# A four-stage block on one core: gates, scaling and table switches reordered in six places

## The chip, the cores and the metric

The kernel runs on one core of a Trainium2 chip. The metric is the device time in microseconds of one execution; smaller is better. Times given are medians of several runs. One further execution was recorded by the hardware profiler, and all durations of single instructions come from it.

## The reference, cut to what matters

The input x has 4 rows of 512 tokens with 512 channels in fp32. A side input f of the same shape drives four gates. The reference is two layers of two steps each:

```python
x = x + mamba2(gate(x, f, f, w0, u0, cond))        # L0: attn
x = x + experts(gate(x, f, f, w1, u1, cond))       # L0: 8 experts, top 2, with gate
x = x + attention(gate(x, f, f, w2, u2, cond))     # L1: 16 heads in 4 groups, causal
x = x + ffn(gate(x, f, f, w3, u3, cond))           # L1: silu(g) * u, 1408 wide

def gate(r, k, v, w, u, time_emb):                 # k = v = f
    decay = exp(-exp(w)) * (0.5 + 0.5 * tf)        # one number per row and channel
    ek = exp(min(k, 30)); ekv = ek * v
    # scans over the tokens, forwards and backwards, of ekv and of ek
    num = nf + nb - ekv + exp(min(u + k, 30)) * v
    den = df + db - ek + exp(min(u + k, 30))
    return sigmoid(r) * num / max(den, 1e-8) * (0.8 + 0.2 * tf)

# mamba2: z, xBC, dt = h @ in_proj; xBC = silu(conv4(xBC)); y by chunks with
# cumulative sums of dA = softplus(dt) * A; then
y = y * silu(z)
y = y * rsqrt(mean(y * y) + eps) * norm_w
return y @ out_proj.T
```

Everything of a gate except sigmoid(r) depends on f alone, so a gate's quotient can be made long before x is there.

## The kernel before, in words

Channels or tokens lie on the 128 partitions; every product is an fp32 matmul of 128 by 128 with up to 512 columns. The program is written as one stream, and a scheduler orders each engine's instructions from it. `after(engine, ...)` pins what is inside it behind the last instruction issued so far on those engines. The class `Tables` (`act`) does the same for ScalarE's function tables: `act.use(name)` issues a table load behind everything recorded under the old table, and each call `act(...)` is pinned behind the load. A raw `nc.scalar.activation` is not pinned, and where it meets another table the compiler puts a load in front of it.

**Gates.** `gate_pair` makes the quotient of two chunks of 128 channels of one row as a generator: loads and Exp of k (`keys`), ek times k (`products`), a forward scan (L256) and a backward scan (L262) for the numerator and for the denominator, the bonus with exp(u + k) (L273 to L277), Ln and Exp for the reciprocal on ScalarE, three operations of 128x1024 on VectorE (L319, L323, L328), and for all but row 0 of the first gate a store of 512 KB to memory (L330, on SP's queue). A row of one gate is two pairs. `make_gates` interleaves consecutive pairs; `pump()` runs it up to its next mark, five marks to a pair, `nudge()` runs it one step. `gated` loads the stored quotient and multiplies it by tanh(x / 2) + 1; `have` first pumps until that gate is made. The list for the second layer is the four rows of gate 2, then the four of gate 3.

**Start.** Row 0's first gate is made from the beginning: its two pairs run six steps each, issued one pair after the other in the program and interleaved by the scheduler. The weights wxb, wzt and wot (2 MB, L926) are loaded; POOL makes the diagonal tiles `skip` (L921). Then each pair is finished, multiplied by the tanh (L1275), and its half of the products of the first eight chunks is issued (`conv_products`, L1007). Taps on ScalarE and VectorE (L1022) follow, `time_steps` (dt and dA, small operations on VectorE), and `sums`: three products of dA with triangles (ppr), Exp, a copy cs (L991), a transpose of cs on TensorE (pcs, L993), its copy csT (L995) and a store, from which the tiles lm are loaded again, spread over partitions.

**Rows.** For each row b and each tile t of 128 tokens: `start_tile`, `start_scores`, `decays`, `outputs`, `squares`, `norm`, and for the tile before (`old`) `turn`, `project`, `scale`, `add_x`. `turn` transposes y and multiplies by norm_w as it leaves PSUM: the first four of eight blocks by one VectorE operation (L1219), the others by four on ScalarE (L1227). `project` multiplies by wot (L1235). One table switch to Silu and one back is in each tile. `pump` makes the later gates of layer 0 in between, and `routing` steps through `choose_experts` (gate 1, logits) and `route` for the row before: ranks and slots by small VectorE operations and products such as ptok (L576), whose two inputs ov and os are built on VectorE. The tables that `route` needs (lane, res_id, place, v_lo, v_e) are made on POOL and VectorE near the beginning (L437 to L464).

**Experts.** Token rows are gathered by expert into blocks. `moe.round()` does one block: products pg, pn and po (L775, L786, L808) with weights loaded on SP's queue, 3 MB a block at most. From block 17 on, two slots of weights alternate. In `more`, each round is followed by one `pump()`, now for the second layer's gates, until block NBLK - 4. Then the results of row 0 are combined with x (L1454 to L1464).

**Attention.** Four groups of 4 heads; for each group, 4 rows; 64 heads in all. `begin` issues the products of the next head, `scores` the softmax of a head (mask L1585, maximum L1587, a nudge of the gates, Exp L1592 as raw activation, L1593, L1594), `context` and `dense` the rest. In group 0, at the second head of row b, the results of row b + 1 are combined and its gated input is made (`gated(2, b + 1)`). Then the FFN, by rows, with its Silu at L1700.

Of the kernel before, what the change touches and what calls it, by code (L numbers as in the profile page):

```python
# [80 lines left out]
def block_kernel(ctx: ExitStack, tc: tile.TileContext, a: dict, out: bass.AP):  # L81
# [354 lines left out]

    lane = count("lane", [[1, P]])  # L437

    res_id = [count(f"res{c}", [[TOPK * T, B], [P, NT]], 1, 1 + c * T) for c in range(2)]
    for r in res_id:  # L440
        for b in (0, B - 1):
            rb = r[:, b * NT : (b + 1) * NT]
            nc.vector.tensor_scalar(rb, rb, float(AT[b] - b * TOPK * T), None, ALU.add)

    places = tmp.tile([P, NBLK], I32, tag="th", name="places")
    for lo, hi in ((0, FIRST), (FIRST, NBLK - NEARLY)):
        half = (hi - lo + 1) // 2
        nc.gpsimd.iota(places[:, lo : lo + 2 * half], pattern=[[1, half], [half, 2]], base=lo,  # L450
                       channel_multiplier=0)
    place = rt.tile([P, NBLK - NEARLY], F32, name="place")
    nc.vector.tensor_copy(place, places[:, : NBLK - NEARLY])
    e_nq = count("e_nq", [[NQ, E]])
    v_id = count("v_id", [[1, 1]], 1)

    v_lo = rt.tile([P, 1], F32, name="v_lo")
    v_e = rt.tile([P, 1], F32, name="v_e")
    jk = rt.tile([P, E], F32, name="jk")
    nc.vector.tensor_tensor(jk, sel, e_nq, ALU.mult)  # L460
    nc.vector.tensor_reduce(v_e, jk, AX.X, ALU.add)
    nc.vector.tensor_tensor(v_lo, v_id, v_e, ALU.subtract)
    nc.vector.tensor_scalar(v_lo, v_lo, float(P), None, ALU.mult)
    nc.vector.tensor_scalar(v_e, v_e, 1.0 / NQ, 1.0 - E, ALU.mult, ALU.add)  # L464


# [39 lines left out]

    def route(lg, b, fine):
        n = NT * E
# [56 lines left out]
        yield  # L565
        pt = ps_tp("ptok")
        over = lambda v: v.unsqueeze(2).to_broadcast([P, NT, P])
        lanes = lane.unsqueeze(1).to_broadcast([P, NT, P])
        for c, (q, s_) in enumerate(vq):
            ov = tmp.tile([P, NT, P], F32, tag="th", name="ov")  # L570
            nc.vector.tensor_tensor(ov, lanes, over(q), ALU.is_equal)
            nc.vector.tensor_tensor(ov, ov, over(res_id[c][:, bt_]), ALU.mult)
            os_ = tmp.tile([P, NT, P], F32, tag="th", name="os")
            nc.vector.tensor_tensor(os_, lanes, over(s_), ALU.is_equal)
            for t in range(NT):
                nc.tensor.matmul(  # L576
                    pt[:, :P], lhsT=ov[:, t, :], rhs=os_[:, t, :],
                    start=(t == 0 and c == 0), stop=(t == NT - 1 and c == 1),
                )
# [15 lines left out]
    def choose_experts(b, xb, parts, pool, fine=False, **kw):  # L595

        lg = rt.tile([P, NT, E], F32, tag="lg", name="lg", bufs=2)
        nt = NT // parts
        for i in range(parts):
            h = gated(1, b, xb, pool, slice(i * nt * P, (i + 1) * nt * P), **kw)  # L600
            if fine:
                yield
            logits(h, b, lg, i * nt, nt)
            yield
        yield from route(lg, b, fine)

# [254 lines left out]
    with ExitStack() as ph:  # L861
# [23 lines left out]
        def lend_halves():  # L885
# [9 lines left out]
        lent = [  # L895
            {"f": lend("y", 3), "eu": lend("tmp", 2)},
            {
# [5 lines left out]
        pairs = [gate_pair(0, 0, c0, first, lent[c0 // 2]) for c0 in range(0, NC, 2)]  # L903
        for pair in pairs:
            for _ in range(6):
                for _ in step(pair):
                    pass
        x = {0: load_x(0)}
        turned, lend_turned = [], lend_halves()
        for cc in range(NC):  # L910
            turned.append(lend_turned())
            act(turned[cc], x[0][:, cc, :], AF.Tanh, scale=0.5)
        act.use(act.LOG_EXP)
        NX = DPROJ - DI
        wxb = wx.tile([P, NC, NX], F32, name="wxb")
# [8 lines left out]
        for k in range(NC):  # L924
            nc.sync.dma_start(out=wzt[:, k, :], in_=a["in_projT"][k * P : (k + 1) * P, :DI])
        nc.sync.dma_start(out=wot, in_=a["out_projT"].rearrange("(k p) m -> p k m", p=P))  # L926

        def time_steps(w):
# [44 lines left out]
        def sums(w):  # L973
# [14 lines left out]
            nc.vector.tensor_tensor(dte, dt, ex[:, 1], ALU.mult)  # L988

            cs = sm.tile([P, n], F32, tag="cs", name="cs", bufs=2)  # L990
            nc.vector.tensor_copy(cs, pp[:, :n])  # L991
            pcs = ps_tp("pcs")
            nc.tensor.transpose(pcs[:n, :P], cs, ident)  # L993
            csT = four[:n, 0:2, :].rearrange("p i t -> p (i t)")
            nc.vector.tensor_copy(csT, pcs[:n, :P])  # L995
            nc.sync.dma_start(out=cs_d[w.b], in_=csT)
# [213 lines left out]
        def turn(u):  # L1210

            u.yT = sm.tile([P, NDI, P], F32, tag="yT", name="yT")
            for hh in range(2):
                pyt = ps_tp("pyt")
                for j in range(4):
                    js = slice(j * P, (j + 1) * P)
                    nc.tensor.transpose(pyt[:, js], u.y[hh][:, js], ident)
                if hh == 0:
                    nc.vector.tensor_tensor(  # L1219
                        u.yT[:, :4, :],  # L1220
                        pyt.rearrange("p (j t) -> p j t", t=P),
                        col("norm_w", 0, 4).unsqueeze(2).to_broadcast([P, 4, P]),
                        ALU.mult,
                    )
                else:
                    for j in range(4):
                        nc.scalar.mul(  # L1227
                            u.yT[:, 4 + j, :], pyt[:, j * P : (j + 1) * P], col("norm_w", 4 + j)
                        )

# [63 lines left out]
        load_sums(w, 0, 1)  # L1294
        decays(u, 0)
        old = None
        routing = iter(())
        for b in range(B):
# [6 lines left out]
            for t in range(NT):  # L1305
# [86 lines left out]
                with after(*ENGINES):  # L1392
                    next(routing, None)
                    if b == B - 1 and t == 1:
                        next(routing)
# [75 lines left out]
    with tc.tile_pool(name="moe_w2", bufs=1, reuse_waits="tile") as wm:  # L1471
# [4 lines left out]
        def more(limit):  # L1476
            while moe.i < min(limit, moe.known):
                moe.round()
                if moe.i < NBLK - NT:
                    with after(nc.vector):  # L1480
                        pump()

# [28 lines left out]
    with att as ph:  # L1511
# [64 lines left out]
        def scores(u, i, qT):  # L1576

            prs = []
            for qi in range(NT):
# [11 lines left out]
                rsum = sm.tile([P, 1], F32, tag="rsum", name="rsum", bufs=4)  # L1591
                nc.scalar.activation(pr, psc[:, :n], AF.Exp, bias=nmax, accum_out=rsum)  # L1592
                nc.vector.reciprocal(rsum, rsum)  # L1593
# [50 lines left out]
        def begin(n):  # L1644
# [5 lines left out]
            return groups[g, b], queries(groups[g, b], i)  # L1650

        groups = {}
        ready, held = begin(0), None
        for n, (g, b, i) in enumerate(heads_):
            u, qT = ready
            if g == 0 and i == 1 and b + 1 < B:
                combine(b + 1)
                hs[b + 1] = gated(2, b + 1, x[b + 1], gp, tag="h", name=f"h2_{b + 1}")
            if n + 1 < len(heads_):
                ready = begin(n + 1)  # L1660
            prs = scores(u, i, qT)
            if held is not None:
# [7 lines left out]
        for _ in making:  # L1670
            pass


    with ExitStack() as ph:
# [9 lines left out]
        for b in range(B):  # L1684
            h = gated(3, b, x[b], gp, tag="h", name=f"h3_{b}")
            hd = []
            for i in range(NFF):
# [11 lines left out]
                hi = sm.tile([P, T], F32, tag="hd", name="hd", bufs=NFF + 2)  # L1699
                nc.scalar.activation(hi, pg, AF.Silu, scale=col("gate_s", i))  # L1700
                nc.vector.scalar_tensor_tensor(hi, pu, col("up_s", i), hi, ALU.mult, ALU.mult)  # L1701
# [85 lines left out]
```

## Time and profile before

| | |
|---|---|
| median of 3 runs | 2587.08 us (2586.99 to 2592.27) |
| profiled execution | 2591.44 us, span 2589.7 |
| mean granted TensorE clock | 0.978 |
| TensorE busy | 2446.0 us |
| VectorE, ScalarE, POOL busy | 1409.8, 1032.3, 250.4 us |
| table loads on ScalarE | 68 of 1.283 us |
| stores of gate quotients (L330) | 30 of 512 KB, five of them in 860 to 1180 us |

The stages lie one behind the other: start to about 100 us, rows to about 750, experts to about 1180, attention to about 2140, FFN to the end. In these rows, "busy" is the time in which an engine executes; a wait is an idle time of an engine just before an instruction, and "<-" names what released it. "PEclk" is the clock that TensorE was granted, in tenths. In the timeline, the first column is the start in us from the span's start, the second the duration, and a bracket at the end gives the idle time before.

### The profile page before, as it was taken

To read this page: it belongs to the slowest core of one execution; us is meant where nothing else is said; L and a number is where in the kernel's file an instruction comes from. 1 tells how busy PE (TensorE), PEld (TensorE's weight loads), DVE (VectorE), ACT (ScalarE), POOL (GpSimd) and SP (SyncE) were. 2 spreads that over 40 slices of the span, in tenths; PEclk is the share of its full clock that TensorE was granted. 3 is DMA by queue.
4 is the path that set the end of the run, shared out by engine and by line. 5 is a ranking of instruction groups with operands and counts; after the bars stand their busy time and mean duration, and the time that the engine had idled before them with its cause. 6 is when DMAs were issued, how large, how long until landed. Compare 5 with 4: busy or idle time off the path is not lost.

```text
span 2589.7 us, 24584 instructions
## 1 busy us (share of the span) xinstructions
PE 2446.0 (94%) x8204; PEld 1301.0 (50%) x8204; DVE 1409.8 (54%) x2786; ACT 1032.3 (40%) x2129; POOL 250.4 (10%) x301
## 2 busy tenths in 40 slices
PE   3889998999999999999989999999999999999999
PEld 1555555556544444445545555555555554444444
DVE  8789998997335555646686554556544441010010
ACT  4666756657222333325554444344443431000000
POOL 1031323313211111120000000000000000000000
PEclk9979998999899999999999999999999999999999
DMA  6222523324244697745231101110000012000000
GB/s 217 77 94 76 188 69 112 131 80 159 66 175 140 223 337 283 274 177 163 75 92 46 46 27 29 45 45 30 21 25 17 17 69 82 17 0 16 8 8 16
DMA packets 88510, 244.09 MB, mean 94 GB/s; under 512 B 9536, under 2 KB 19136, under 8 KB 79296
## 3 DMA queue, kind: packets, MB, share of 16 engines
q1 hardware_dynamic: 79200, 215.78, 24.3%
q0 software_dynamic: 6880, 22.55, 2.5%
q10 hardware_dynamic: 2304, 4.20, 0.4%
q8 instruction: 65, 1.06, 0.2%
q14 instruction: 61, 0.50, 0.1%
HBM read 284.82 MB, written 47.05 MB: 128 GB/s over the span
## 4 chain that ended last, share of the span: by engine, by line
PE 75%; DVE 16%; ACT 4%; DMA 3%; issue 1%; POOL 0%; SPq 0%; ACTq 0%; DVEq 0%
PE pd L1629 8%; PE pq L1565 7%; PE pfu L1696 6%; PE pfo L1706 6%; PE pfg L1691 6%; PE pctx L1614 5%; PE po L808 5%; PE pg L775 5%; PE pn L786 5%; PE psc L1582 3%; PE pc L1007 2%; PE po L1235 2%; PE pv L1551 2%; PE ptp L1605 2%; PE pz L1078 2%; PE pk L1543 2%
## 5 line engine op out<-in xcount | busy, mean ns | idle before, releaser
L1565 PE MATMUL pq<-h,wq 128*128 128x512 f32 x512 | 248.0, 600 | 10.9 <-ACT pr L1592 10.9
L1629 PE MATMUL pd<-cx,wd 128*128 128x512 f32 x512 | 222.9, 593 | 1.3 <-DVE xr L1637 1.3
L1007 PE MATMUL pc<-h,wxb 128*128 128x512 f32 x320 | 151.6, 629 | 46.1 <-DVE h L1275 39.0
L1700 ACT ACTIVATE hd<-pfg,cols 128x512 f32<-128x512 f32 x44 | 30.3, 688 | 380.8 <-PE pfg L1691 380.8
L1701 DVE SCALAR_TENSOR_TENSOR hd<-pfu,cols,hd 128x512 f32<-128x512 f32 x44 | 33.0, 751 | 269.1 <-PE pfu L1696 269.0
L1585 DVE TENSOR_TENSOR psc<-psc,mask 128x128 f32<-128x128 f32 x256 | 72.2, 288 | 192.9 <-PE psc L1582 192.9
L1592 ACT ACTIVATE pr<-psc,nmax 128x128 f32<-128x128 f32 (+3 forms) x256 | 135.5, 530 | 95.6 <-DVE nmax L1587 94.9
L1614 PE MATMUL pctx<-pT,v 128*128 128x512 f32 (+3 forms) x512 | 153.6, 443 | 8.5 <-ACT pT L1608 5.1
L1696 PE MATMUL pfu<-h,ffu 128*128 128x512 f32 x352 | 158.7, 592 | 0.8 <-DMA ffu<-in_upT 0.8
L1691 PE MATMUL pfg<-h,ffg 128*128 128x512 f32 x352 | 158.6, 592 | 0.0
L1582 PE MATMUL psc<-kT,qT 128*128 128x128 f32 (+3 forms) x512 | 153.1, 439 | 3.1 <-ACT qT L1573 1.6
L1629 PEld LDWEIGHTS pd<-cx,wd 128*128 128x128 f32 x512 | 95.9, 190 | 116.8 <-issue 110.0
L1706 PE MATMUL pfo<-hd,ffd 128*128 128x512 f32 x352 | 151.7, 592 | 0.0
L775 PE MATMUL pg<-w,hT 128*128 128x512 f32 x312 | 144.7, 606 | 4.3 <-DMA w<-in_w1x 4.3
L1614 PEld LDWEIGHTS pctx<-pT,v 128*128 128x128 f32 x512 | 93.4, 190 | 99.6 <-issue 35.9
L808 PE MATMUL po<-w,yT 128*128 128x512 f32 x312 | 142.3, 596 | 1.2 <-DMA w<-in_w2x 1.2
L786 PE MATMUL pn<-w,hT 128*128 128x512 f32 x312 | 140.7, 592 | 0.0
L1637 DVE TENSOR_TENSOR xr<-xr,pd 128x512 f32<-128x512 f32 x64 | 44.0, 687 | 169.3 <-PE pd L1629 169.3
L1587 DVE TENSOR_REDUCE nmax<-psc 128x1 f32<-128x128 f32 (+3 forms) x256 | 124.0, 486 | 2.6
L1007 PEld LDWEIGHTS pc<-h,wxb 128*128 128x128 f32 x320 | 62.6, 201 | 119.6 <-issue 73.8
L1565 PEld LDWEIGHTS pq<-h,wq 128*128 128x128 f32 x512 | 87.1, 192 | 69.4 <-issue 56.1
L1605 PEld LDWEIGHTS ptp<-ident,pr 128*128 128x128 f32 x640 | 77.8, 142 | 87.4 <-issue 38.4
(308 smaller groups left out, 4220.2 us busy)
## 6 DMA issues: line engine op xcount, KB each, us to landing
w<-in_w1x SPq DMA_DIRECT2D x80, 1024.0 KB
w<-in_w2x SPq DMA_DIRECT2D x40, 1024.0 KB
wb<-in_b1x SPq DMA_DIRECT2D x40, 512.0 KB
lm<-cs SPq DMA_DIRECT2D x32, 512.0 KB
kt<-in_fT SPq DMA_DIRECT2D x62, 256.0 KB
ek<-ek SPq DMA_DIRECT2D x62, 256.0 KB
ekv<-ekv SPq DMA_DIRECT2D x62, 256.0 KB
g<-num SPq DMA_DIRECT2D x30, 512.0 KB
```

The source lines that it names most:

```text
L775: nc.tensor.matmul(pg, lhsT=hT[:, k, :], rhs=self.w1[s][0][:, k, :], start=(k == 0), stop=(k == NC - 1))
L786: nc.tensor.matmul(pn, lhsT=hT[:, k, :], rhs=self.w1[s][1][:, k, :], start=(k == 0), stop=(k == NC - 1))
L808: nc.tensor.matmul(po, lhsT=yT[:, j, :], rhs=self.w2[s][:, j, :], start=(j == 0), stop=(j == NI - 1))
L1007: nc.tensor.matmul(pc, lhsT=wxb[:, k, m * P : (m + 1) * P], rhs=h[:, k, :], start=(k == 0), stop=(k == NC - 1),)
L1565: nc.tensor.matmul(pq, lhsT=u.wq[:, k, i * KVC : (i + 1) * KVC], rhs=u.h[:, k, :], start=(k == 0), stop=(k == NC - 1),)
L1582: nc.tensor.matmul(psc[:, :n], lhsT=qT[:, qi * P : n], rhs=u.kT[:, :n], start=True, stop=True)
L1592: nc.scalar.activation(pr, psc[:, :n], AF.Exp, bias=nmax, accum_out=rsum)
L1614: nc.tensor.matmul(pctx[:, kj * P :], lhsT=u.v[:, kj, :], rhs=pT[:, kj, kj * P :], start=(kj == 0), stop=(kj == NT - 1),)
L1629: nc.tensor.matmul(po, lhsT=u.wd[:, i, m * P : (m + 1) * P], rhs=u.ctxT[i], start=(i == 0), stop=(i == HPG - 1),)
L1691: nc.tensor.matmul(pg, lhsT=wg[:, k, cs], rhs=h[:, k, :], start=(k == 0), stop=(k == NC - 1))
L1696: nc.tensor.matmul(pu, lhsT=wu[:, k, cs], rhs=h[:, k, :], start=(k == 0), stop=(k == NC - 1))
L1706: nc.tensor.matmul(po, lhsT=wdn[:, i, m * P : (m + 1) * P], rhs=hd[i], start=(i == 0), stop=(i == NFF - 1),)
```

## The change

It has seven parts.

1. The tables of the routing are made behind the first tile's first `decays` on VectorE instead of near the beginning.
2. Row 0's first pair of the first gate is finished, on VectorE's order, before the second pair's six steps are issued. Its ekv tiles are lent from another pool.
3. wot is multiplied by norm_w once, by eight POOL operations of 128x512. `turn` then only copies, one ScalarE operation of 128x512 for each half.
4. In `sums`, the transposed cumulative sums come from a fourth product with dA in place of a transpose of cs.
5. In `route`, for the rows that are routed in fine steps, ov and os of the first half are made in a tile of another pool, and a step ends there; the PSUM tile of ptok is taken behind it. The last row's loop therefore takes an additional routing step at two tiles instead of one.
6. In the experts' stage, `pump` is called with one and two by turns.
7. In the attention, Exp goes through `act` under the table that also holds Ln; the table is loaded at its start. `gated(2, b + 1)` moves from the second head to the third, behind `begin`, between two table switches. The FFN's Silu goes through `act`, its table asked for at the end of the attention.

```diff
@@ route
-        pt = ps_tp("ptok")
+        pt = None
         for c, (q, s_) in enumerate(vq):
-            ov = tmp.tile([P, NT, P], F32, tag="th", name="ov")
+            if fine and c == 0:
+                both = pool.tile([P, 2, NT, P], F32, **kw)
+                ov, os_ = both[:, 0], both[:, 1]
+            else:
+                ov = tmp.tile([P, NT, P], F32, tag="th", name="ov")
+                os_ = tmp.tile([P, NT, P], F32, tag="th", name="os")
...
+            if fine and c == 0:
+                yield
+            if pt is None:
+                pt = ps_tp("ptok")
@@ start of row 0
-            {"f": lend("y", 3), "eu": lend("tmp", 2)},
+            {"f": lend("y", 3), "eu": lend("tmp", 2), "ekv": lend("xc", NDI)},
...
-        for pair in pairs:
+        def six_steps(pair):
             for _ in range(6):
                 for _ in step(pair):
                     pass
+
+        six_steps(pairs[0])
         x = {0: load_x(0)}
...
         act.use(act.LOG_EXP)
+
+        with after(nc.vector):
+            for _ in pairs[0]:
+                pass
+            six_steps(pairs[1])
...
+        for k in range(NDI):
+            nc.gpsimd.tensor_scalar(wot[:, k, :], wot[:, k, :], col("norm_w", k), None, ALU.mult)
@@ sums
+            nc.tensor.matmul(
+                pp[:n, 3 * n : 3 * n + P], lhsT=dA.rearrange("p t h -> p (t h)"), rhs=tri_le,
+                start=True, stop=True,
+            )
             cs = sm.tile([P, n], F32, tag="cs", name="cs", bufs=2)
             nc.vector.tensor_copy(cs, pp[:, :n])
-            pcs = ps_tp("pcs")
-            nc.tensor.transpose(pcs[:n, :P], cs, ident)
             csT = four[:n, 0:2, :].rearrange("p i t -> p (i t)")
-            nc.vector.tensor_copy(csT, pcs[:n, :P])
+            nc.vector.tensor_copy(csT, pp[:n, 3 * n : 3 * n + P])
@@ turn
-                if hh == 0:
-                    nc.vector.tensor_tensor(
...
-                        nc.scalar.mul(
-                            u.yT[:, 4 + j, :], pyt[:, j * P : (j + 1) * P], col("norm_w", 4 + j)
-                        )
+                nc.scalar.copy(
+                    u.yT[:, hh * 4 : (hh + 1) * 4, :].rearrange("p j t -> p (j t)"), pyt
+                )
@@ behind decays(u, 0)
+        with after(nc.vector):
+            lane = count("lane", [[1, P]])
...
@@ loop over rows
-                    if b == B - 1 and t == 1:
+                    if b == B - 1 and t < 2:
                         next(routing)
@@ more
-                        pump()
+                        pump(1 + moe.i % 2)
@@ attention
-                nc.scalar.activation(pr, psc[:, :n], AF.Exp, bias=nmax, accum_out=rsum)
+                act(pr, psc[:, :n], AF.Exp, bias=nmax, accum_out=rsum)
...
+        with after(nc.scalar):
+            act.use(act.LOG_EXP)
...
             if g == 0 and i == 1 and b + 1 < B:
                 combine(b + 1)
-                hs[b + 1] = gated(2, b + 1, x[b + 1], gp, tag="h", name=f"h2_{b + 1}")
             if n + 1 < len(heads_):
                 ready = begin(n + 1)
+            if g == 0 and i == 2 and b + 1 < B:
+                act.use(act.EXP)
+                hs[b + 1] = gated(2, b + 1, x[b + 1], gp, tag="h", name=f"h2_{b + 1}")
+                act.use(act.LOG_EXP)
...
+        act.use(act.SILU)
@@ FFN
-                nc.scalar.activation(hi, pg, AF.Silu, scale=col("gate_s", i))
+                act(hi, pg, AF.Silu, scale=col("gate_s", i))
```

More of the change, by code (lines that the diff above doesn't have):

```diff
@@ L435, in count @@
         return tf_
[L437 to L464, printed above, removed]
     N2 = B * NT
@@ L505, in logits, with route @@
             nc.sync.dma_start(out=rows_h[lo : lo + P, :], in_=hr)
-    def route(lg, b, fine):
+    def route(lg, b, fine, pool, **kw):
         n = NT * E
@@ L565, in route @@
         yield
-        pt = ps_tp("ptok")
         over = lambda v: v.unsqueeze(2).to_broadcast([P, NT, P])
         lanes = lane.unsqueeze(1).to_broadcast([P, NT, P])
+        pt = None
         for c, (q, s_) in enumerate(vq):
-            ov = tmp.tile([P, NT, P], F32, tag="th", name="ov")
+            if fine and c == 0:
[4 more added lines that the diff above has]
+                os_ = tmp.tile([P, NT, P], F32, tag="th", name="os")
             nc.vector.tensor_tensor(ov, lanes, over(q), ALU.is_equal)
             nc.vector.tensor_tensor(ov, ov, over(res_id[c][:, bt_]), ALU.mult)
-            os_ = tmp.tile([P, NT, P], F32, tag="th", name="os")
             nc.vector.tensor_tensor(os_, lanes, over(s_), ALU.is_equal)
+            if fine and c == 0:
+                yield
+            if pt is None:
+                pt = ps_tp("ptok")
             for t in range(NT):
@@ L604, in choose_experts @@
             yield
-        yield from route(lg, b, fine)
+        yield from route(lg, b, fine, pool, **kw)
     taken = rt.tile([P, 1], F32, name="taken")
@@ L1217, in turn @@
                     nc.tensor.transpose(pyt[:, js], u.y[hh][:, js], ident)
-                if hh == 0:
[L1219 to L1223, printed above, removed]
-                    )
-                else:
-                    for j in range(4):
-                        nc.scalar.mul(
-                            u.yT[:, 4 + j, :], pyt[:, j * P : (j + 1) * P], col("norm_w", 4 + j)
-                        )
+                nc.scalar.copy(
+                    u.yT[:, hh * 4 : (hh + 1) * 4, :].rearrange("p j t -> p (j t)"), pyt
+                )
         def project(u):
@@ L1295, in block_kernel @@
         decays(u, 0)
+        with after(nc.vector):
+            lane = count("lane", [[1, P]])
+            res_id = [count(f"res{c}", [[TOPK * T, B], [P, NT]], 1, 1 + c * T) for c in range(2)]
+            for r in res_id:
+                for b in (0, B - 1):
+                    rb = r[:, b * NT : (b + 1) * NT]
+                    nc.vector.tensor_scalar(rb, rb, float(AT[b] - b * TOPK * T), None, ALU.add)
+            places = tmp.tile([P, NBLK], I32, tag="th", name="places")
+            for lo, hi in ((0, FIRST), (FIRST, NBLK - NEARLY)):
+                half = (hi - lo + 1) // 2
+                nc.gpsimd.iota(places[:, lo : lo + 2 * half], pattern=[[1, half], [half, 2]], base=lo,
+                               channel_multiplier=0)
+            place = rt.tile([P, NBLK - NEARLY], F32, name="place")
+            nc.vector.tensor_copy(place, places[:, : NBLK - NEARLY])
+            e_nq = count("e_nq", [[NQ, E]])
+            v_id = count("v_id", [[1, 1]], 1)
+            v_lo = rt.tile([P, 1], F32, name="v_lo")
+            v_e = rt.tile([P, 1], F32, name="v_e")
+            jk = rt.tile([P, E], F32, name="jk")
+            nc.vector.tensor_tensor(jk, sel, e_nq, ALU.mult)
+            nc.vector.tensor_reduce(v_e, jk, AX.X, ALU.add)
+            nc.vector.tensor_tensor(v_lo, v_id, v_e, ALU.subtract)
+            nc.vector.tensor_scalar(v_lo, v_lo, float(P), None, ALU.mult)
+            nc.vector.tensor_scalar(v_e, v_e, 1.0 / NQ, 1.0 - E, ALU.mult, ALU.add)
         old = None
```

## The prediction, made before the changed kernel was run

> **What bounds the kernel now.** The profile's busy rows come first: TensorE works 2446.0 of 2589.7 us, so no change of this size can come from anything but the 144 us in which it idles and the time in which its clock is halved.
>
> ```profile
> PE 2446.0 (94%) x8204; PEld 1301.0 (50%) x8204; DVE 1409.8 (54%) x2786; ACT 1032.3 (40%) x2129; POOL 250.4 (10%) x301
> ...
> DVE  8789998997335555646686554556544441010010
> ...
> PEclk9979998999899999999999999999999999999999
> ```
>
> One slice is 64.7 us. VectorE is 80 to 90% busy in the first ten slices (the mamba rows), and there PEclk falls below 9: gaps of TensorE are followed by stretches at half clock. In 60 to 1180 us I count 13 such stretches, 99 us long together (49 us of work lost beside some 58 us of gaps); from 1180 on three of 3.4 to 6.8 us.
>
> Second, the waits of TensorE, before 1180 us and from there to 2140 us (line, what it waits for, total us, times, longest):
>
> ```profile
> PE pc L1007 <- DVE h L1275: 39.0, 1, 39.0
> PE pp L1094 <- DVE yT L1219: 7.9, 3, 4.8
> ...
> PE ptok L576 <- DVE ov L572: 4.7, 4, 1.9
> ...
> PE pg L775 <- DMA w<-in_w1x: 4.3, 2, 3.8
> PE pcs L993 <- DVE cs L991: 3.0, 3, 1.8
> ```
> ```profile
> PE pq L1565 <- ACT pr L1592: 10.9, 5, 2.5
> PE ptp L1605 <- DVE pT L1608: 6.4, 4, 3.3
> ```
>
> The reader sees that each of the change's targets (L1219, the ptok and pcs products, the attention's L1592) is there, and is a few us. Third, the timeline around one of the 2.5 us waits for L1592 (start, duration, engine, line):
>
> ```profile
> 1529.19 1.28 ACT L121 ACT_TABLE_LOAD   x1
> ...
> 1530.48 1.15 ACT L121 ACTIVATE rec<-rec,tiny 128x1024 f32<-128x1024 f32 x1
> 1531.65 1.28 ACT L1592 ACT_TABLE_LOAD   x1
> 1532.95 0.37 ACT L1592 ACTIVATE pr<-psc,nmax 128x128 f32<-128x128 f32 x1
> ...
> 1533.46 1.98 PE L1565 MATMUL pq<-h,wq 128*128 128x512 f32 x4 [2.50 <-ACT pr L1592]
> ```
>
> A gate's Ln (L121) fetches one table, the softmax's Exp the other, and the head's first softmax row comes 3.7 us late.
>
> **The change part by part** (against the profiled execution, 2591.4 us).
>
> *Start.* VectorE is busy 20.00 of 20 us in 20 to 40 us, and TensorE's first product waits for h at 42.35. With the first pair's steps first, I add VectorE's instructions in the new order by their rows (scans 1.2, bonus 0.68, the three of the end 1.25 each): its h comes at about 36, the second pair's at 51 instead of 47.8. TensorE starts 6 us earlier, but the first eight chunks' products, which ran without a break from 42.35 to 77.8, are 35 us in all, so their first half lasts to 54 and the second follows it without a gap. The taps (L1022, VectorE) then free the last bank about 3 us earlier (75 for 78), while the gate steps left behind (4.6 us of backward scan and bonus) come between the small operations of time_steps: dA at about 91 for 91.87. The tables' 14 small VectorE operations (2.3 us) now stand between the first tile's products, where VectorE is idle 5.7 us in pieces. Sum: -2.
>
> To it comes the scaling of wot: 8 POOL operations of 128x512 behind the 2 MB load, issued at 24.1, whose bytes come by about 40. The nearest POOL row of this shape is L1181 with 1.04 alone: 8 to 12 us, wanted by the first project at 142. That is hidden[...]. The row:
>
> ```profile
> 150.37 1.04 POOL L1181 TENSOR_TENSOR st<-st,ex 128x512 f32<-128x512 f32 x1 [2.14 <-PE pyo L1159]
> ...
> 150.46 3.16 DVE L256 TENSOR_TENSOR_SCAN den<-decay,ek 128x512 f32<-128x512 f32 x2
> ```
>
> Two scans take 2.4 alone and 3.16 beside one POOL operation: the first began 0.09 us behind it and took 2.04 instead of 1.21. [...] by the row of skip (L921, 8 operations in the same crowded stretch) nothing. About ten of these us lie before the taps: I take +2. Start: 0 (-4 to +7).
>
> *Rows, 100 to 860 us.* turn()'s L1219 (0.68 x 16 = 11 us) leaves VectorE; ScalarE gets 32 copies of 128x512 (0.58 by L125's zs row) = 18.6 for 64 x 0.365 = 23.4. The case with 4.8 us of wait:
>
> ```profile
> 428.14 0.72 ACT L258 ACTIVATE f<-num,fall 128x511 f32<-128x511 f32 x1 [1.17 <-DVE num L256]
> ...
> 429.11 0.68 DVE L1219 TENSOR_TENSOR yT<-pyt,cols 128x512 f32<-128x512 f32 x1
> ...
> 429.85 0.80 PE L1094 MATMUL pp<-xc,xc 128*128 128x128 f32 x2 [4.78 <-DVE yT L1219]
> ```
>
> L1219 stood behind a scan and L328 (1.2 each) on VectorE while ScalarE was idle 1.17 us: a copy there would have ended about 2 to 4 us sooner. Of 7.9 + 1.0 us of waits for L1219 I take 7 off, and of the half clock of 6.8 us around it 1.5. pcs: the fourth product of sums() needs only dA, so the 3.0 us of L991 go, but the copy of csT stays on VectorE and the load of lm behind it: 1.5 off. ptok: 4.7 + 1.7 us; the ov/os of the first half now are made one step earlier, but the second half's still come before its products: 2 off. Against it: the doubled routing step of the last row, its one additional table load (1.28) and ScalarE's queue in place of VectorE's: +2. Rows: -10 (-22 to +4).
>
> *Experts, 860 to 1180 us.* pump(1 + i % 2) makes 8 pairs of the later gates there instead of 5. VectorE has 5 x 0.69 of its own in a round of 11.2 us, and a pump is about 3.6: two pumps with the round's 3.5 are 10.7, just under it. What can hurt is SP's queue, where each pair's store stands before weight loads:
>
> ```profile
> 862.20 1.23 DVE L328 SCALAR_TENSOR_TENSOR num<-den,num 128x1024 f32<-128x1024 f32 x1
> ...
> 863.46 0.34 SPq L330 DMA_DIRECT2D g<-num  x1
> ...
> 864.53 0.35 SPq L708 DMA_DIRECT2D w<-in_w1x  x1
> ...
> 871.02 1.19 PE L775 MATMUL pg<-w,hT 128*128 128x512 f32 x1 [3.75 <-DMA w<-in_w1x]
> ```
>
> The load could be issued only after the gate's end, and TensorE idled 3.75 us and ran 6.8 at half clock. Of five stores that one cost 7.1; the waits on w1 and w2 with it sum to 5.5. Three more pairs bring 3 stores and 18 loads of 256 KB (6 MB in all, in a stretch that moves 263 GB/s): at the mean, (5.5 + 3.4) x 8/5 = 14, so +5.3; some are covered, +4. Bounds: -3 (the store at 863 falls elsewhere) to +12.
>
> *Attention.* Three gains. (a) Pairs of table loads inside a head: groups 1 to 3 have five waits of 2.44 to 3.28 us at them, 13.4 in all. After, only h2_1 to h2_3's gating and the start have loads; the pairs' Ln and Exp run under the table that the softmax uses. -13.4, and -2 of small ones, -1.7 of the half clock at 1607. (b) In group 0, two pairs are finished in a burst, since the gating of row 1 wants (2,1), then (2,2), (2,3), not yet made: VectorE is busy 20.00 in 1300 to 1320, and 0.92 + 0.39 + 1.41 + 3.39 us of gaps with 3.4 lost to the clock follow. With 8 pairs made before, all of these exist: -9.5, and -2.4 for the loads at 1294. (c) Against: the switch to LOG_EXP at the start falls between the tanhs of the first h (two loads, 2.57, before its last two): +2.5; three gatings with two loads each in line with the head's Exp: 3 x 1.5 = +4.5. Together -22; I take -21 (-28 to -12). [...] the trace shows the 1283, and the Ln 0.01 us behind it[...].
>
> *FFN.* The Silu preload moves a load that 1.28 us already hid: 0.
>
> Sum: 0 - 10 + 4 - 21 = -27: 2564.4 for the profiled execution, which stood 4.4 above the median of 2587.1; so 2560.
>
> **The rivals.**
>
> A, the gain is eaten in the experts (the other sign). Each of 8 stores stands before the w1 load of a block, waits for VectorE's gate end, and costs what the one at 863 did, 3.75 + 3.4 = 7.1. With n costly stores for one it is (n - 1) x 7.1, less the +4 already booked: 24 for five, 31 for six. It decides from six on, where the 27 are gone (2591); with seven it is +39, 2599. For it: w1's slot alternates, and one block's load is asked for two rounds ahead only. Against it: four of five stores cost nothing or 0.5.
>
> B, the new loads and the gating in line take the attention's gain: the gating moved behind begin(n+1) stands ahead of the head's softmax on ScalarE with 2.6 of loads, 2.5 of tanh. Each of three at 5 instead of 1.5, the start at 5 instead of 2.5: +13, 2573.
>
> C, the rows don't gain: when L1219 goes, the next wait in line (scans, y L1172, 5.6 us once) takes its place: +10, 2570.
>
> D, with the gaps go more of the half-clock stretches that follow them than I booked. Of 49 us lost, a quarter: -12, 2548.
>
> E, nothing moves since the gains are covered: within 5 us of 2587.
>
> **How the numbers follow.** Forecast 0.38, B 0.16, C 0.16, D 0.15, A 0.09, E 0.06. Range: D's far end and the rows' -22 give about 2535, B and C together 2583; A and E lie outside with the lower tail: about 2 in 10. Measurements of this kernel tell 0.2% (5.2 us) from nothing: E is the 0.06 within it, A the 0.09 slower, the rest, 0.85, faster.
>
> **What would show it.** Right: no wait of TensorE for ACT pr L1592 above 1 us in 1400 to 2140, no wait for yT over 2 us, ACT_TABLE_LOAD from 68 to 61, first product at about 36 us with ppr at 91; 8 gate stores before 1180. Wrong: waits on w<-in_w1x above 10 us in 860 to 1180 (A), waits for L1592's successor at three places in group 0 (B), TensorE's idle time in 100 to 660 still the 36.5 us that its busy times of 179.9, 188.9 and 154.7 leave (C), a first product later than 40. The estimate is wrong above all if VectorE is late for the experts' y with two pumps in a round.

## The result and the profile after

The changed kernel takes 2577.9 us (median of 6 executions, 2574.5 to 2584.4), the kernel before 2587.0 (6, 2584.1 to 2592.3): a ratio of 0.9969, interval 0.9954 to 0.9984. It is faster by 9 us and not by the 27 of the forecast. The profiled execution took 2576.2 us. That is 15.2 us less than the one before, which stood 4.4 us above its median: part of what the two profiles differ by is scatter.

The busy rows of the changed kernel:

```profile
PE 2441.6 (95%) x8208; PEld 1298.7 (50%) x8208; DVE 1410.2 (55%) x2782; ACT 1014.4 (39%) x2078; POOL 276.8 (11%) x309
...
DVE  8789999996345676746664665555434441010010
...
PEclk9889999999999999999999999999999999999999
```

VectorE is busier in the experts' stage (slices 12 to 17) and has lost the 8 of slice 21, in the attention's first group; the clock of the rows is higher. Where the time went is read from five points that both traces have: the first ppr (end of the start), the first pg (end of the rows), the first pk (end of the experts' stage), the first pfg (end of the attention), and, inside the experts' stage, the start of the last routing's products pidx (797.6 us before, 780.6 after). Times are those of one profiled execution each.

| stage | before | after | difference | forecast |
|---|---|---|---|---|
| start to first ppr | 92.2 | 93.8 | +1.6 | 0 |
| rows, ppr to pg | 585.8 | 567.2 | -18.6 | -10 |
| experts, pg to pk | 487.1 | 512.5 | +25.4 | +4 |
| attention, pk to pfg | 965.7 | 941.8 | -23.9 | -21 |
| FFN | 458.9 | 459.2 | +0.3 | 0 |

All of the +25.4 lies behind pidx: 367.5 us before, 392.9 after. In this stretch TensorE's idle time went from 7.3 to 25.9 us, and the work lost to the half clock from 3.4 to 8.5 (mean granted clock 0.99 and 0.98). TensorE's waits after, up to 1180 us:

```profile
PE pc L998 <- DVE h L1257: 32.7, 2, 31.8
PE pg L754 <- DMA w<-in_w1x: 13.7, 6, 5.3
...
PE po L787 <- DMA w<-in_w2x: 4.5, 4, 1.7
PE pp L1085 <- ACT yT L1209: 4.5, 3, 2.4
PE pg L754 <- ACT hT L727: 4.2, 1, 4.2
```

and from 1180 us on:

```profile
PE pq L1577 <- ACT pr L125: 2.2, 2, 1.8
PE psc L1594 <- ACT pr L125: 1.4, 2, 1.2
```

The waits for yT have gone from 8.9 to 4.5 us and those of pq for the softmax from 10.9 to 2.2 (with 2.6 of pk for it, which are new); no wait for pr above 0.5 us is left behind 1350 us. In their place stand 13.7 + 4.5 = 18.2 us for weights, where there were 5.5. One of them in the timeline of the changed kernel:

```profile
830.97 1.20 DVE L328 SCALAR_TENSOR_TENSOR num<-den,num 128x1024 f32<-128x1024 f32 x1
...
832.20 0.34 SPq L330 DMA_DIRECT2D g<-num  x1
...
832.95 0.34 SPq L687 DMA_DIRECT2D w<-in_w1x  x1
...
840.26 2.05 PE L754 MATMUL pg<-w,hT 128*128 128x512 f32 x2 [5.29 <-DMA w<-in_w1x]
```

This is the pattern of 863 us before: the weights' load is issued 9.3 us after its block's first product (823.6), behind the gate's end on VectorE and the store on SP. The second new wait is ScalarE's:

```profile
802.77 1.15 ACT L313 ACTIVATE rec<-den,tiny 128x1024 f32<-128x1024 f32 x1 [0.76 <-DVE den L273]
...
803.94 1.28 ACT L121 ACT_TABLE_LOAD   x1
...
805.23 1.15 ACT L121 ACTIVATE rec<-rec,tiny 128x1024 f32<-128x1024 f32 x1
...
806.40 1.28 ACT L121 ACT_TABLE_LOAD   x1
...
807.69 1.06 ACT L121 ACTIVATE rec<-rec 128x1024 f32<-128x1024 f32 x1
808.65 0.58 ACT L780 ACTIVATE yT<-pyt 128x512 f32<-128x512 f32 x1
809.13 0.58 ACT L727 COPY hT<-pfl 128x512 f32<-128x512 f32 x1
...
809.76 2.93 PE L754 MATMUL pg<-w,hT 128*128 128x512 f32 x3 [4.18 <-ACT hT L727]
```

The reciprocal of a gate pair with its two table loads is 5.9 us in one piece on ScalarE, and the block's two copies stand behind it.

### The profile page after: what moved, and what is told of

It reads as the page before. It is cut to its first block, busy times and chain, and to the rows that moved or that the text cites. A ratio compares the mean times of both kernels' runs of the same rounds, so it can differ in the third digit from the quotient of the medians.

```text
span 2574.5 us, 24554 instructions
## 1 busy us (share of the span) xinstructions
PE 2441.6 (95%) x8208; PEld 1298.7 (50%) x8208; DVE 1410.2 (55%) x2782; ACT 1014.4 (39%) x2078; POOL 276.8 (11%) x309
## 4 chain that ended last, share of the span: by engine, by line
PE 73%; DVE 16%; DMA 4%; ACT 3%; issue 2%; POOL 1%; SPq 0%; DVEq 0%; ACTq 0%; POOLq 0%
PE pd L1641 8%; PE pq L1577 7%; PE pfu L1715 6%; PE pfo L1725 6%; PE pfg L1710 6%; PE pctx L1626 5%; PE pg L754 4%; PE pn L765 4%; PE po L787 4%; PE psc L1594 4%; PE pv L1563 2%; PE pk L1555 2%; PE pc L998 2%; PE ptp L1617 2%; DVE xc L1013 2%; PE po L1217 2%
## 5 line engine op out<-in xcount | busy, mean ns | idle before, releaser
L754 PE MATMUL pg<-w,hT 128*128 128x512 f32 x312 | 150.5, 626 | 17.8 <-DMA w<-in_w1x 13.7
L1585 ACT ACTIVATE qT<-pq 128x512 f32<-128x512 f32 x64 | 38.2, 597 | 234.8 <-PE pq L1577 234.1
```

Of the source, the lines that this page charges most:

```text
L754: nc.tensor.matmul(pg, lhsT=hT[:, k, :], rhs=self.w1[s][0][:, k, :], start=(k == 0), stop=(k == NC - 1))
```

## The experiments

Executions of one kernel that ran twelve times or more differ by 11 to 19 us (the kernel before: 2578 to 2593); in the rows, the profiles show between 21 and 39 us of work lost to the half clock (mean granted clock 0.93 before, 0.95 after). So two numbers are given for each: the ratio of the medians, and the stages of one profiled execution. Each kernel computes the whole reference.

| kernel | median, us | ratio to before (interval) | first ppr | rows | pidx to pk | attention |
|---|---|---|---|---|---|---|
| before | 2584.3 to 2587.1 | 1 | 92.2 | 585.8 | 367.5 | 965.7 |
| after | 2577.9 | 0.9969 (0.9954 to 0.9984) | 93.8 | 567.2 | 392.9 | 941.8 |
| after, one pump | 2583.8 | 0.9994 (0.9984 to 1.0004) | 94.0 | 566.8 | 365.5 | 973.1 |
| after, stores on POOL | 2578.5 | 0.9963 (0.9949 to 0.9978) | 93.5 | 574.1 | 388.4 | 943.1 |
| after, loads on POOL | 2589.7 | 1.0017 (1.0009 to 1.0025) | 95.3 | 574.2 | 406.6 | 941.9 |
| after, both on POOL | 2560.0 | 0.9904 (0.9879 to 0.9928) | 94.1 | 566.9 | 377.1 | 940.9 |
| after, both on POOL, scaling meant to come later | 2568.0 | 0.9921 (0.9903 to 0.9938) | 95.2 | 573.2 | 380.9 | 939.9 |
| after, both on POOL, later pumps | 2556.5 | 0.9880 (0.9863 to 0.9896) | 96.4 | 575.2 | 365.0 | 944.9 |
| after, both on POOL, later pumps, wot scaled on ScalarE | 2550.5 | 0.9866 (0.9848 to 0.9884) | 89.3 | 571.0 | 366.8 | 944.1 |
| after, old start | 2586.5 | 1.0009 (0.9995 to 1.0023) | 95.1 | 565.6 | 393.7 | 941.9 |
| before, part 6 alone | 2608.4 | 1.0089 (1.0072 to 1.0106) | 92.1 | 580.3 | 391.6 | 957.2 |
| before, part 7 alone | 2593.3 | 1.0035 (1.0024 to 1.0046) | 92.2 | 580.1 | 367.6 | 970.9 |
| before, part 3 alone | 2589.7 | 1.0024 (1.0014 to 1.0033) | 97.0 | 573.8 | 365.4 | 967.6 |
| before, part 3 with ScalarE | 2583.8 | 0.9991 (0.9982 to 1.0000) | 93.0 | 578.1 | 366.3 | 967.2 |
| before, part 4 alone | 2590.4 | 1.0028 (1.0015 to 1.0041) | 93.3 | 578.8 | 366.9 | 970.3 |
| before, parts 1 and 2 alone | 2585.2 | 1.0002 (0.9994 to 1.0010) | 89.4 | 586.4 | 366.9 | 970.2 |
| before, both on POOL | 2576.8 | 0.9964 (0.9952 to 0.9976) | 93.8 | 576.6 | 359.9 | 968.4 |

**The pumps.** Part 6 undone in the changed kernel:

```diff
-                        pump(1 + moe.i % 2)
+                        pump()
```

> The changed kernel with one pump in every round of the experts' stage (part 6 undone). The experts' stage, from its first product pg to the attention's first pk, took 487.1 us before and 512.5 after. Theory (the doubled pumps cost it): 487 to 490 us, waits of TensorE on w1 and w2 back to about 5.5 us of the 18.2 after, while the attention, which must again finish pairs in a burst in group 0, takes about 952 instead of 941.8: in all 2563. Rival (the loss comes from the stage's other start, 17 us earlier against its loads and routing): the experts' stage stays above 505 us, and the time is not below 2578.

The stage behind pidx is back at 365.5 us and the waits for weights at 5.0. But the attention is at 973.1, 21 us more than the theory said, and the median, 2583.8, is no gain. The timeline shows where, in group 0:

```profile
1327.38 1.06 ACT L125 ACTIVATE rec<-rec 128x1024 f32<-128x1024 f32 x1
...
1330.92 1.22 DVE L328 SCALAR_TENSOR_TENSOR num<-den,num 128x1024 f32<-128x1024 f32 x1
...
1340.22 2.68 DVE L383 SCALAR_TENSOR_TENSOR h<-th,h 128x512 f32<-128x512 f32 x4 [6.82 <-DMA h<-g]
...
1342.20 1.28 ACT L112 ACT_TABLE_LOAD   x1
...
1344.00 1.22 PE L1555 MATMUL pk<-h,wkv 128*128 128x512 f32 x1 [21.02 <-ACT pr L125]
```

The gate that the gating wants isn't made: its last pair is finished, stored and loaded again (8 us from L328 to the product with it), and the switch back to the softmax's table waits behind the tanh. The head's Exp and with it TensorE wait 21 us. The same pair of parts from the other side, in the kernel before:

> The kernel before with part 6 alone (one and two pumps by turns). Theory (the loss and the gain both belong to the pumps): the experts' stage 510 to 514 instead of 487.1, the attention about 10 us less than its 965.7, in all 2600. Rival (the loss comes of both the pumps and the other parts): the stage stays below 500 and the time below 2590.

> The kernel before with part 7 alone (Exp under the table with Ln, gating behind begin, between two switches). From the first pk to the first pfg the attention took 965.7 us before, 941.8 after, 973.1 with part 7 but one pump in the experts' stage. Theory (part 7 needs the pairs that part 6 makes early; without them the pairs that the gating asks for are finished in line with the softmax, in one wait of about 20 us): 970 to 976, the time 2592 to 2597. Rival (part 7 takes the waits at the table loads by itself, and the 21 us wait belongs to something else of the changed kernel): 945 to 952, the time 2566 to 2572.

Part 6 alone costs 24.1 us behind pidx and saves 8.5 in the attention: 2608.4, 8 more than expected. So the loss in the experts' stage belongs to the pumps, whatever else is changed. Part 7 alone has the same wait as the changed kernel with one pump (26.7 us for pk <- pr in all, the longest 21.1) and is slower than before, 2593.3. So neither part is a gain alone. Together they shorten the attention by 24, but their sum with the experts' +25 is nothing, until the experts' stage is mended. The burst of group 0 belongs to part 6, as forecast; that without the pairs part 7 turns it into a wait three times as long was not.

**SP's queue.** The stores, then the loads, then both were issued from POOL in the changed kernel:

```diff
-            nc.sync.dma_start(out=gts[l][b][:, c0 : c0 + 2, :], in_=g)
+            (nc.gpsimd if l >= 2 else nc.sync).dma_start(
+                out=gts[l][b][:, c0 : c0 + 2, :], in_=g
+            )
```

(the loads of kt, ek and ekv in the same way).

> The changed kernel with the stores of gates 2 and 3 issued from POOL instead of SP, so that no weight load stands behind them. Theory (stores ahead of the loads on SP's queue): waits on w1 and w2 fall from 18.2 to about 6 us, the experts' stage from 512.5 to about 498, the time to 2564. Rival (two pumps in a round overfill VectorE and ScalarE, whatever the queue): the waits on weights fall little or turn into waits for hT and yT, and the stage stays at 508 to 514.

> The changed kernel with the gate loads of the second layer (kt, ek, ekv) on POOL and the stores left on SP. The stage from pidx to pk took 392.9 us after, 388.4 with the stores alone on POOL, 377.1 with both. Theory (the loads, which wait for a buffer that VectorE frees, hold the weights up as the stores do): 380 to 384. Rival (only both together help, since either one is enough to block a load): 387 or more.

> As the run with the stores on POOL, and the loads of kt, ek and ekv of gates 2 and 3 on POOL too. Theory (gate transfers of any kind hold up SP's queue, since the loads wait for a buffer that VectorE frees): the stage falls further, to about 492. Rival (POOL's queue then holds up the gathers of hb and the scatters of o): waits of pfl for hb appear, and the stage is at 505 or more.

The waits of TensorE in the experts' stage, for w1 and w2 and for hT and yT, in us:

| | weights | hT, yT | pidx to pk |
|---|---|---|---|
| before | 5.5 | none shown | 367.5 |
| before, both on POOL | 1.8 | none shown | 359.9 |
| after | 18.2 | 6.1 | 392.9 |
| stores on POOL | 10.8 | 10.6 | 388.4 |
| loads on POOL | 18.9 | 12.9 | 406.6 |
| both on POOL | 1.0 | 11.8 | 377.1 |

Both together take 15.8 us off, the stores alone 4.5, and the loads alone make it 13.7 worse. The stores' run met its rival: the stage from pg to pk took 508.1, and the waits for hT and yT rose as those for weights fell. The theory that each kind holds the weights up on its own missed too: one kind left on SP is enough to block the weights, which is what the rival of the loads' run said. SP's own waits for VectorE between 780 and 1180 us show it. With the stores moved, SP stands before the gate loads for 80.6 us (58.0 in the changed kernel):

```profile
SPq L246 <- DVE num L256: 43.7, 8, 8.8
SPq L237 <- DVE eu L275: 36.9, 6, 11.9
```

With the loads moved, it stands before the stores for 86.4 us (38.1 in the changed kernel):

```profile
SPq L330 <- DVE num L328: 86.4, 8, 15.0
```

The load that came at 832.95 us in the changed kernel has its like in both other kernels. With the loads alone moved the store is still in front of it, and it is issued 9.3 us after its block's first product:

```profile
839.01 1.20 DVE L328 SCALAR_TENSOR_TENSOR num<-den,num 128x1024 f32<-128x1024 f32 x1
...
840.24 0.34 SPq L330 DMA_DIRECT2D g<-num  x1
840.98 0.34 SPq L687 DMA_DIRECT2D w<-in_w1x  x1
...
847.03 1.19 PE L754 MATMUL pg<-w,hT 128*128 128x512 f32 x1 [4.03 <-DMA w<-in_w1x]
```

With both moved it goes out 3.6 us after that product (822.99), as soon as the block's last pg has read the old weights, and TensorE does not wait for it:

```profile
822.99 3.60 PE L756 MATMUL pg<-w,hT 128*128 128x512 f32 x8
...
826.62 0.34 SPq L689 DMA_DIRECT2D w<-in_w1x  x1
...
831.84 0.56 POOL L330 DMA_DIRECT2D g<-num  x1 [4.06 <-DVE num L328]
```

Why the loads alone on POOL lose 13.7 isn't settled; behind pidx 17.1 us were lost to the half clock for 8.5 after, and TensorE was idle 32.4 us for 25.9. Its profiled execution was the slowest of twenty, but the median, 2589.7, is 12 above the changed kernel's too. POOL as the issuing engine cost little: with both moved, an issue from POOL took 0.54 to 0.56 us in the median and at most 0.76, for 0.32 to 0.33 in the median from SP, and TensorE's waits for hb, which POOL gathers, were 2.9 us in the second sample of that kernel for 3.1 after. The kernel before has the same defect in small:

> The kernel before with the gate transfers of the second layer on POOL, all else as before. Theory (with one pump a round SP's queue cost the waits on weights that the profile shows, 5.5 us, and the half clock behind one, 3.4): the stage from pidx to pk 360 to 362 instead of 367.5, the time 2578 to 2581. Rival (POOL's queue costs the gathers as much): 366 or more, the time 2587 or more.

Seven to eight us less behind pidx, 2576.8 in all: this one edit of the old kernel is worth as much as the whole change.

The four kernels together tell what belongs to the queue (us from pidx to pk):

| | one pump | one and two by turns |
|---|---|---|
| gate transfers on SP | 367.5 | 392.9 |
| gate transfers on POOL | 359.9 | 377.1 |

Of the +25.4, 17.2 remain where no gate transfer is on SP's queue (21.0 with the second sample of "both on POOL", 380.9), and only 8.2 go with the queue. The 15.8 us that moving both takes off hold these 8.2 and the 7.6 that the queue cost already before.

**ScalarE's waits.** In the 17.2 us the trace shows ScalarE. The changed kernel with both on POOL has these waits of TensorE, where the kernel before with both on POOL has none of them:

```profile
PE pg L756 <- ACT hT L729: 7.3, 4, 4.8
PE po L789 <- ACT yT L782: 4.5, 2, 4.2
```

The longest two, at 809.1 and 1044.6 us, lie behind the same burst as above, and around each a stretch of 6.8 us at half clock begins (in the changed kernel, behind the same wait at 809.76, the mean granted clock is 0.75 in 810 to 820 us, and the eight pg take 6.28 us for 3.60). The second of them:

```profile
1037.53 1.15 ACT L313 ACTIVATE rec<-den,tiny 128x1024 f32<-128x1024 f32 x1 [0.76 <-DVE den L273]
...
1043.94 0.58 ACT L782 ACTIVATE yT<-pyt 128x512 f32<-128x512 f32 x1
```

11.8 us of waits and 6.8 us of work lost to the clock cover the 17.2; no run takes the burst itself off ScalarE, so this is read from the trace and not tested. With both on POOL the second pump was moved behind block 17, where weights have two slots:

```diff
-                        pump(1 + moe.i % 2)
+                        pump(1 + (moe.i > NEARLY and moe.i % 3 > 0))
```

> All gate transfers of the second layer on POOL, and the second pump only behind block 17, there in two rounds of three (about as many pumps in all). Between the last routing product pidx and the first pk the stage took 367.5 us before, 392.9 after, 377.1 with the transfers on POOL and the changed kernel's pumps; what is left there are waits for hT and yT, 11.8 us, the largest at block 9. Theory (a round with two pumps overfills ScalarE, in any block): these waits move behind block 17 and stay at 8 to 14 us, the stage at 374 to 380, the time 2558 to 2562. Rival (it is the early blocks, with one slot of weights, that can't bear a second pump): the waits fall below 5 us, the stage to 368 to 371, the time to 2552.

The waits for hT and yT fell from 11.8 to 3.8 and the stage to 365.0, as the rival said and a little better; none is above 0.8 us. But that it is the single slot of weights isn't shown. With the pumps by turns, 5.8 of the 11.8 us lie behind block 17 (892 us), where there are two slots, the wait at 1044.6 among them. And the later pumps finish seven pairs in this stretch instead of eight; the attention takes 944.9 for 940.9. So a part of the 12.1 us is work moved on. The rest may come from where in a round the burst falls; the two were not taken apart. The medians, of four executions each, are 2556.5 here and 2560.0 and 2568.0 in the two kernels with both on POOL.

**The start and part 3.** Parts 1 and 2 were undone in the changed kernel and then run alone; part 3 was run alone with the scaling on POOL and on ScalarE; in the last run the scaling was to come later. The theory of the last two is that POOL's eight operations hold VectorE up in the start.

> The changed kernel with parts 1 and 2 undone (tables near the beginning, both pairs' steps interleaved). The first ppr came at 92.2 us before and 93.8 after, the rows behind it took 567.2 after. Theory (the start's new order brings nothing by itself): ppr at 92 to 93, rows 566 to 569, the time 2575 to 2578. Rival (the tables' later place is what relieves the rows, or the first pair ahead pays): rows 573 or more, the time 2584 or more.

> The kernel before with parts 1 and 2 alone (tables late, first pair ahead). With parts 1 and 2 undone in the changed kernel the profiled execution lost 1.6 us but the median of twelve rose by 8. Theory (the two parts bring something only in making good the scaling's hold-up): ppr at 90.5 to 92, the rows as before, 580 to 586, the time 2583 to 2588. Rival (the tables' later place relieves the rows by itself): rows 575 or less, the time 2577 to 2580.

> The kernel before with part 3 alone (wot scaled by norm_w on POOL, one ScalarE copy for each half). From the first ppr to the first pg of the experts the rows took 585.8 us before and 567.2 after. Theory (VectorE's 0.68 and its place in the queue): 576 to 579, and the waits for yT of 8.9 fall to about 4.5, the time 2578. Rival (POOL's scaling and ScalarE's longer copies give it back): 584 to 588, the time 2587.

> The kernel before with part 3 alone, its scaling on ScalarE instead of POOL. With POOL's scaling the first ppr came at 97.0 us for 92.2 before, the rows took 573.8, and the time was 2589.7. Theory [...]: ppr at 92 to 93, rows 572 to 580, the time 2578 to 2581. Rival (the copies on ScalarE are no gain in the rows, and the start has nothing to do with it): the time 2584 or more.

> All gate transfers of the second layer on POOL, and the scaling of wot behind the first tile's decays instead of in the start. With the scaling in the start the first ppr comes at 93.8 to 94.1 us, at 97.0 where part 3 is alone, 92.2 before. Theory [...]: ppr at 90.5 to 92, the rows unchanged, the time 2557. Rival (they hold up nothing, and the later ppr has another cause): ppr at 93.5 to 94.5, or the later place delays the first project and the rows lose 3 us or more, the time 2560 to 2564.

Parts 1 and 2 alone bring ppr to 89.4 us, 2.8 sooner; part 3 alone makes it 97.0, 4.8 later; both in the changed kernel 93.8, +1.6, near their sum of +2.0. These are single profiles, and ppr scatters: kernels with the old start and no scaling on POOL have 92.1 to 93.8, with the old start and that scaling 95.1 and 97.0, with the new start and no scaling on POOL 89.3 and 89.4, with both 93.5 to 96.4. The two effects stand clear of that, their sizes only roughly. Part 3 alone also missed in its time: the rows, 573.8, are better than its theory, the median, 2589.7, is worse than its rival. Behind ppr parts 1 and 2 alone show no gain (rows 586.4, 1.0002). In the changed kernel without them the profile has 1.3 us more at ppr, and the median 8.6 us more; the profiled execution was the fastest of the twelve, and the stages do not say where the others lost theirs. That difference stays open. The run that was to put the scaling behind the first decays did not move it: the profile has it at 43.9 us instead of 42.8. It is another sample of the kernel with both on POOL, and says nothing on its question.

The scaling on ScalarE does:

```diff
-            nc.gpsimd.tensor_scalar(wot[:, k, :], wot[:, k, :], col("norm_w", k), None, ALU.mult)
+            nc.scalar.mul(wot[:, k, :], wot[:, k, :], col("norm_w", k))
```

ppr comes at 93.0 for 97.0, and 2583.8 for 2589.7. The theory was right as to the hold-up; the time lies between what the two said, so the rows of part 3 bring less than I took them to, about 2 us net with the start undisturbed (0.9991, an interval that ends at 1). The timeline of the changed kernel shows the hold-up, beside POOL's eight operations:

```profile
42.76 8.29 POOL L915 TENSOR_SCALAR wot<-wot,cols 128x512 f32<-128x512 f32 x5 [34.97 <-DMA wot<-in_out_projT]
...
44.50 1.61 DVE L319 SCALAR_TENSOR_TENSOR st<-st,yT 128x1024 f32<-128x1024 f32 x1 [1.56 <-ACT yT L125]
...
47.77 1.59 DVE L328 SCALAR_TENSOR_TENSOR h<-st,num 128x1024 f32<-128x1024 f32 x1
```

The same two take 1.22 us each where POOL is idle (the timeline of the 21 us wait has L328): 0.4 us lost on each. Of the eleven VectorE operations that begin beside POOL's eight, seven are longer by 0.4, 2.9 us in all, which is less than the 4 us or more by which ppr moves. What the rest is isn't shown. POOL's own times vary too: in part 3 alone, one of the eight took 5.95 us, for a median of 2.06; what held it isn't shown.

**The best of these.** All that helped in one kernel, its scaling on ScalarE on the theory, again, that POOL's eight operations hold VectorE up in the start:

> As the run with the gate transfers on POOL and the second pump behind block 17, and the scaling of wot by eight ScalarE operations in place of POOL's, in an idle stretch of ScalarE at 45 to 50 us. Theory [...]: ppr at 90 to 91 us instead of 93.8 to 96.4, the rows as they were (567 to 575), the time 2552. Rival (the scaling's place does not matter, or ScalarE's Exp of the next gate pair comes late behind it): ppr at 93.5 or later, the time 2556 or more.

2550.5 us, 0.9866 (0.9848 to 0.9884), against 0.9969 of the change: about 27 us more. ppr is at 89.3, the stage behind pidx at 366.8 for 392.9, with seven pairs in it here too.

**Part 4 alone.**

> The kernel before with part 4 alone (csT by a fourth product with dA). Theory: the waits of pcs for cs (3.0 us) go, of which half is given back: rows 584 instead of 585.8, the time 2585 to 2587, not to be told from before. Rival (the earlier store of the sums brings lm sooner, and decays with it): rows 578 or less.

2590.4: slower by 0.28%, which neither said. The rows of its profile, 578.8, lie within what other kernels with the old rows have (576.6 to 586.4), and its first ppr, 93.3, within the scatter named above; no cause is shown. Part 5 was not run alone.

## Why the prediction was wrong, point by point

**The experts' step failed**, and with it the sum. It priced the additional pairs by SP's queue alone, in proportion to the five before: "(5.5 + 3.4) x 8/5 = 14, so +5.3; some are covered, +4". Measured: +25.4. The queue's part of that is 8.2, not far from the 5.3. The other 17.2 remain with the queue free, and they are the term that was put at nothing: ScalarE. "Two pumps with the round's 3.5 are 10.7, just under it" counted VectorE alone; ScalarE's 5.9 us of reciprocal and table loads, in order before the block's copies, were in no term of the sum, though the rows at 1529 us, quoted for the attention, show their parts. In the trace, waits for hT and yT (11.8) and the half clock at them (6.8) are as large as the 17.2. For the weights the proportion was too low as well: with eight stores for five TensorE waited on weights ten times instead of three, and the gate loads on the same queue, counted as bytes only, block it as the stores do.

**Rival A** named the queue and its place, with "24 for five, 31 for six" costly stores on top of the +4. The stage's excess over the +4 is 21.4, near its 24, but that is chance: in its terms the queue's 8.2 are little more than one more costly store (7.1), and ScalarE is not in it. It missed that the gate loads matter too: moving the stores alone gives back 4.5 us only. Its sign, waits on w1 above 10 us, came with 13.7, of which 8.4 lie behind 860 us.

**The attention** was right in sum, -23.9 for -21, and against the five other kernels with the old attention and one pump (967.2 to 970.3) about -27. No wait for pr above 0.5 us is left behind 1350, and the table loads went from 68 to 61, as said. "-9.5" for the burst was right as to size: part 6 alone gives 8.5. Not seen was that part 7 without it is a loss (970.9 for 965.7; 973.1 in the changed kernel with one pump), where its terms sum to a gain of 12; the forecast held since both parts are there. Rival B did not come true.

**The rows**, -10 forecast, were 18.6 less by the two profiled executions. But the profile before is at the upper end: six profiled executions with the old rows (one of them with part 4) have 576.6 to 586.4, median 580; nine with the changed rows have 565.6 to 575.2, median 571. That is -9, so about half of the -18.6 comes from the profile that it was taken against. yT's waits fell by 4.4 of the 7 us that I took off, and one of 2.4 us is left where none above 2 was to be. The half clock fell by more than I took. Rival C's sign did not come: TensorE's idle time in 100 to 660 us is 31.6 for 36.5.

**The start** was 0 with a range of -4 to +7, and came at +1.6: -2.8 from parts 1 and 2 (forecast -2) and +4.8 from the scaling (forecast +2). The first product came at 35.1 us, as said (36). The +2 was an estimate between one scan that took 0.83 us longer beside a POOL operation and the row of skip, from which I took none. Measured beside POOL's eight, seven of eleven VectorE operations are longer by about 0.4 us each, and the eight took 14.0 us instead of 8 to 12.

With +25 in place of +4 the forecast would have been 2581, for 2577.9 measured.

## What to carry to other kernels

Work moved into a stage where the busiest engine is full was paid for here by the queues of that stage, in which it stood ahead of the stage's own work (a load of weights behind a gate's store went out 9.3 us after its block's first product, 3.6 with the gate transfers on POOL; a block's two copies stood behind 5.9 us of a gate's reciprocal on ScalarE), so count each queue that the moved work passes (here SP's and ScalarE's), not only the engine with the most work. A transfer that waits for a late result belongs on a queue on which nothing urgent stands behind it; move all such transfers, for here one kind left behind was enough (388.4 and 406.6 us behind pidx with one kind moved, 377.1 with both). To learn what a queue costs, run both edits, the moved work and the freed queue, each with and without the other: moving the queue alone would have put 15.8 us to it where 8.2 of the increase are its own. And two edits can each lose alone where one needs the other, so test a bundle also by taking one part out: the doubled pumps cost 24 us in the kernel before, and the changed kernel is about 6 us faster with them than without.

## What the runs showed of the hardware that was not expected

Eight 128x512 POOL operations beside VectorE took 1.6 to 2.2 us each, and VectorE's 1.22 us operations about 1.6; with part 3 alone one of the eight took 5.95. Issuing a 256 KB load from POOL cost 0.54 to 0.56 us at the median and never over 0.76; VectorE is 63% busy behind pidx in the changed kernel (246.7 of 392.9 us). And the same program varies by 11 to 19 us between executions, while the profiles show between 21 and 39 us lost to the half clock in the rows: changes of 0.3% there can't be read from one profile.
